# Router logits made token-major tile by tile, and the first expert block's rows selected by a one-hot product

## Chip, cores and metric

The kernel runs on one core of a Trainium2 chip. The metric is the device time of one execution, in microseconds (us), the median of three runs. The engines have short names in the profile: PE is the matrix engine, PEld its weight loads (which run beside its products), DVE the vector engine, ACT the scalar engine, POOL the GpSimd engine, SP the engine that issues most of the loads.

## The reference

A network of four layers works on 512 tokens of 768 features in f32. Each layer adds the outputs of a graph part, a mixing part and a feed-forward part to `x`. The change touches the feed-forward parts of layer 0 and layer 2, two mixtures of eight experts in which every token goes to the one expert with the largest logit. The one of layer 2, cut:

```python
x = hidden_states.reshape(-1, d)                 # normalized tokens, 512 x 768
logits = x @ Wg                                  # 768 x 8
probs = jax.nn.softmax(logits, axis=-1)
gate = jnp.max(probs, axis=-1)
expert_idx = jnp.argmax(probs, axis=-1)
h = jax.nn.silu(jnp.einsum('td,edf->etf', x, W1) + b1[:, None, :])   # 8 experts, 768 -> 384
y = jnp.einsum('etf,efd->etd', h, W2) + b2[:, None, :]               # 384 -> 768
combine = jax.nn.one_hot(expert_idx, e, dtype=x.dtype) * gate[:, None]
out = jnp.einsum('te,etd->td', combine, y)
```

Layer 0 has the same with a bias on the logits (`Ws`, `bs`) and gelu.

## The kernel before

Tokens lie in four tiles of 128 (`NT = 4`, `P = 128`). "Token-major" means tokens on the partitions (`xn`, 128 x 4 x 768); "feature-major" means features on the partitions in six chunks (`xnT`, 128 x 6 x 512, `KC = 6`). The routine `moe` (from line 1246) does both mixtures. Its first call, `"f0"` for layer 0, has a bias on the logits and a list of `fill` pieces: products for folding a graph part's weights (line 1787), placed between the routing's steps so that PE has work while DVE routes. Its second call, `"f2"` for layer 2, has no fills; its tokens' mean and spread are known already (`known=True`). The order on each engine is fixed when the program is built; `issue_after(last)` ties some PE pieces into a written order.

A call goes through these steps:

1. The tokens are normalized into `xn`, tile by tile (line 517 in call 1, lines 538 and 540 in call 2). `xn` is also written to memory as `there`, from which rows are gathered later, and in part as `back` (lines 1262 and 1264, from ACT's queue).
2. `to_fm` transposes all 24 128x128 blocks into six PSUM tiles of 512 columns, one per feature chunk, and then copies each out (`copy` alternates between DVE, line 290, and ACT, line 292).
3. `narrow` multiplies the gate's weights, padded to 32 columns, with `xnT` (line 437): the gate is the operand that is loaded, the tokens move, 512 at a time; the six chunks go to four column groups. DVE copies the result to `loT`, in call 1 with the bias. `narrow_tm` then turns it token-major with one product per tile against stacked identities (`fours`), and the logits are copied to `lo` (line 1275).
4. DVE finds each token's expert (maximum, first index), two bf16 products count the tokens per expert (`lower`, `onesb`; they wait for `gb`), and DVE works out `place`, the slot of each token in up to 11 blocks of 128 rows (`NB`), each block belonging to one expert, and `rows`, the row numbers of the blocks' weights. The fills 0 and 1 stand between these products on PE.
5. `spot` (line 1344) is a one-hot matrix in bf16, tokens against all 1408 slots, made tile by tile. 44 small products with token numbers (line 1349) turn it into `who`, the token of each slot. Fill 2 follows on PE.
6. POOL issues the loads with computed addresses, one after another in a written order (`send`): W1 of block 0, the rows of blocks 0 and 1 (`gather`, line 1411, from `there` by `who`), W1 of block 1, W2 of block 0, and so on (`pick`, line 1405).
7. For each block the gathered rows are transposed (`turned`), multiplied by W1 (`first`), transposed and put through the activation (`middle`), and multiplied by W2 (`second`). The block after is prepared meanwhile. Nine blocks always run (`NA`).
8. The results come back to token order and are added to `x`.

`acc` (line 429) is the product helper, `tr` (line 450) the transpose helper; most products in the profile stand under these two lines and are told apart by their tiles. `self.ones` is a 128x128 matrix of ones, `self.fours` four stacked 32x32 identities, `self.col(bs)` the bias with one expert on each partition.

Of the kernel before, what the change touches and what calls it, by code (L numbers as in the profile page):

```python
# [10 lines left out]
F32 = mybir.dt.float32  # L11
# [6 lines left out]
OP = mybir.AluOpType  # L18
# [4 lines left out]
P = 128  # L23
N = 512
NT = N // P
D = 768
KC = D // P
HW = 384
# [177 lines left out]
class Net:  # L206
# [250 lines left out]
    def to_fm(self, x, out):  # L457

        ps = [self.ps() for _ in range(KC)]
        for t in range(NT):  # L460
            for f in range(KC):
                self.tr(ps[f][:, t * P : (t + 1) * P], x[:, t, f * P : (f + 1) * P])
        for f in range(KC):
            self.copy(out[:, f, :], ps[f])

    def to_fm_last(self, x, out):

        nc, cut = self.nc, (NT - 1) * P
        ps = [self.ps() for _ in range(KC)]
        for t in range(NT - 1):  # L470
            for f in range(KC):
                self.tr(ps[f][:, t * P : (t + 1) * P], x[:, t, f * P : (f + 1) * P])
        for f in (0, 1, 3, 4):
            i = nc.scalar.copy(out[:, f, :cut], ps[f][:, :cut])
        with self.tc.issue_after(self.scaled):
            for f in (2, 5):
                nc.vector.tensor_copy(out[:, f, :cut], ps[f][:, :cut])
        for f in range(0, KC, 3):
            p = self.ps()
            for k in range(3):  # L480
                self.tr(p[:, k * P : (k + 1) * P], x[:, NT - 1, (f + k) * P : (f + k + 1) * P])
            at = out[:, f : f + 3, cut:], p[:, :HW].rearrange("p (k n) -> p k n", k=3)
            if f:
                nc.vector.tensor_copy(*at)
            else:
                with self.tc.issue_after(i.ins):
                    i = nc.scalar.copy(*at)
        return i.ins
# [757 lines left out]
    def moe(self, f, act, xn, xnT, wg, bs=None, fill=None, later=None, known=False):  # L1246
# [4 lines left out]
        nc, tc, d = self.nc, self.tc, self.d  # L1251
        E, NA, NB = 8, 9, NT + 7
        with ExitStack() as c:
            one = c.enter_context(tc.tile_pool(name=f + "_one", bufs=1))
            two = c.enter_context(tc.tile_pool(name=f + "_two", bufs=2))
# [6 lines left out]
            nc.scalar.dma_start(there.rearrange("(t p) d -> p t d", p=P), xn)  # L1262

            nc.scalar.dma_start(back[(NA - 1) * P :].rearrange("(t p) d -> p t d", p=P), xn[:, : NB - NA, :])
            self.to_fm(xn, xnT)
            xs = self.chunks(xnT)
            p = self.narrow(wg, xs)
            loT = one.tile([P, N], F32, name="loT")
            if bs is None:
                nc.vector.tensor_copy(loT, p)  # L1270
            else:
                nc.vector.tensor_scalar(loT, p, self.col(bs), None, OP.add)
            lo = one.tile([P, NT, E], F32, name="lo")
            logits = self.narrow_tm(loT, E)
            nc.vector.tensor_copy(lo, logits)
            last = self.told
            if fill:
                with tc.issue_after(last):
                    last = fill(0)
# [12 lines left out]
            p = self.ps()  # L1292
            gf = gb.rearrange("p t e -> p (t e)")
            with tc.issue_after(last):
                self.acc(p[:, :32], [(self.lower, gf)])
                last = self.acc(p[:, 32:64], [(self.onesb, gf)]).ins
            if fill:
                with tc.issue_after(last):
                    last = fill(1)
# [4 lines left out]
            n = cum[:, NT, :]  # L1304
# [16 lines left out]
            at = one.tile([P, NT, E], F32, name="at")  # L1321
# [3 lines left out]
            place = one.tile([P, NT, 1], F32, name="place")  # L1325
# [14 lines left out]
            spot = one.tile([P, NT, NB * P], BF16, name="spot")  # L1340
            io = one.tile([P, NB * P], I16, name="io")
            nc.gpsimd.iota(io, pattern=[[1, NB * P]], base=0, channel_multiplier=0)
            for t in range(NT):
                nc.vector.tensor_scalar(spot[:, t, :], io, place[:, t, :], None, OP.is_equal)
            p = self.ps()
            with tc.issue_after(last):
                for t in range(NT):
                    for i in range(NB):
                        last = nc.tensor.matmul(p[:, 2 * i : 2 * i + 2], spot[:, t, i * P : (i + 1) * P],
                                                self.number[:, t, :], start=t + i == 0,  # L1350
                                                stop=t == NT - 1 and i == NB - 1).ins
            if fill:
                with tc.issue_after(last):
                    last = fill(2)
            sums = one.tile([P, NB], F32, name="sums")
            nc.vector.tensor_reduce(sums, p[:, : 2 * NB].rearrange("p (i a) -> p i a", a=2), AX.X, OP.add)
            who = one.tile([P, NB], I32, name="who")
# [21 lines left out]
            p = self.ps()  # L1379
# [5 lines left out]
            p = self.ps()  # L1385
# [17 lines left out]
            def pick(table, i):  # L1403
                t = self.wp.tile([P, WB], F32, tag="w", name="w") if i < NA else two.tile([P, WB], F32, name="wm")
                return t, nc.gpsimd.indirect_dma_start(
                    out=t, out_offset=None, in_=table.rearrange("e p n -> (e p) n"),
                    in_offset=bass.IndirectOffsetOnAxis(ap=rows[:, i : i + 1], axis=0))

            def gather(i):
                xb = two.tile([P, D], F32, name="xb", bufs=3)  # L1410
                return xb, nc.gpsimd.indirect_dma_start(
                    out=xb, out_offset=None, in_=there, in_offset=bass.IndirectOffsetOnAxis(ap=who[:, i : i + 1], axis=0))
# [4 lines left out]
            def send(fn, *args):  # L1417

                nonlocal sent
                with tc.issue_after(sent) if sent else nullcontext():  # L1420
                    t, i = fn(*args)
                sent = i.ins
                return t

            def turned(xb):
                xbT = two.tile([P, KC, P], F32, name="xbT")
                for k in range(0, KC, 3):
                    p = self.ps()
                    for j in range(3):
                        self.tr(p[:, j * P : (j + 1) * P], xb[:, (k + j) * P : (k + j + 1) * P])  # L1430
                    self.copy(xbT[:, k : k + 3, :], p[:, :HW].rearrange("p (k n) -> p k n", k=3))
                return xbT

            def first(i, xbT, w1):
                p = self.ps()
                w1 = w1.rearrange("p (k n) -> p k n", k=KC)
                self.acc(p[:, :HW], [(xbT[:, k, :], w1[:, k, :]) for k in range(KC)])
                h = two.tile([P, HW], F32, name="h" if i < NA else "hm")
                self.copy(h, p[:, :HW])
                return h  # L1440
# [23 lines left out]
            count = nc.values_load(more[:1], min_val=4, max_val=NB)  # L1464

            w1 = send(pick, W1, 0)
            xb = send(gather, 0)
            ahead = send(gather, 1)
            h = first(0, turned(xb), w1)
            w1 = send(pick, W1, 1)  # L1470
            w2 = send(pick, W2, 0)
            xbT = turned(ahead)
            for i in range(NA - 1):
                hT = middle(i, h)
                h = first(i + 1, xbT, w1)
                if i + 2 < NA:
                    xb = send(gather, i + 2)
                    w1 = send(pick, W1, i + 2)
                after = send(pick, W2, i + 1)
                if i + 2 < NA:  # L1480
                    xbT = turned(xb)
# [7 lines left out]
            with tc.If(count > NA):  # L1489
                for i in range(NA, NB):  # L1490
                    xb, wa, wb = gather(i)[0], pick(W1, i)[0], pick(W2, i)[0]
                    second(i, middle(i, first(i, turned(xb), wa)), wb)
            ys = []
            for t in range(NT):
                ys.append(two.tile([P, D], F32, name="yb", bufs=NT))
                i = nc.gpsimd.indirect_dma_start(out=ys[t], out_offset=None, in_=back,
                                                 in_offset=bass.IndirectOffsetOnAxis(ap=slot[:, t : t + 1], axis=0))
# [11 lines left out]
            last = None  # L1509
# [18 lines left out]
            for t in range(NT):  # L1528
                x = self.x[:, t, :]
                for nb in range(2):  # L1530
                    at = slice(nb * HW, (nb + 1) * HW)
# [1370 lines left out]
```

## Time and profile before

| what | us |
|---|---|
| median of three runs | 3619.51 (3616.93 to 3624.39) |
| the profiled execution's own time | 3622.55 |
| its span | 3620.3 |
| mean granted PE clock | 0.992 |

A page of the profile gives busy times and shares by engine, then groups of instructions. A timeline gives, for each merged group, its start from the start of the span, how long it lasts, engine, line, operation, the tile written and those read, partitions and elements, the number of records (`x12`) and in brackets how long the engine had been idle and what released it. A stretch of time gives the busy time of PE, PEld, DVE, ACT and POOL with the number of instructions, then the granted PE clock (1.00 is full), the share of DMA time and GB/s. The first call's head lies at about 811 to 842 us, the second's at about 2171 to 2205.

### The profile page before, as it was taken

The numbers are of one execution on the slowest core, as the hardware profiler recorded it, in microseconds if no ns is written. First come the engines' busy times: TensorE is split into PE (matmuls) and PEld (weight loads), VectorE is DVE, ScalarE is ACT, GpSimd is POOL, SyncE is SP. The second block draws the span as 40 slices with busy tenths as digits, with TensorE's granted clock in tenths as the row PEclk, the third lists the DMA queues.
The fourth block names the chain that finished last, engine by engine and source line by source line (L and its number), as shares of the span: only waits on it lengthen the run. The fifth ranks groups of instructions, "written<-read, shape, count | busy, mean of one in ns | idle before, by whom it ended". The sixth has DMA issues, their size and how long they took to land. (4 is left out here: it accounts for less than half of the span.)

```text
span 3620.3 us, 40628 instructions
## 1 busy us (share of the span) xinstructions
PE 3526.4 (97%) x15976; PEld 2206.5 (61%) x15981; DVE 1699.7 (47%) x3407; ACT 985.6 (27%) x1753; POOL 475.2 (13%) x522
## 2 busy tenths in 40 slices
PE   8999999999999999999999998999999999999998
PEld 6767666655686675587888885555444444444444
DVE  8647664652523662366777763575222221221211
ACT  3533332432341443142343422363000000000000
POOL 8211110012003010001221213111000000000000
PEclk9999999999999999999999998999999999999999
DMA  4213112228322221032121118415999999999998
GB/s 179 90 50 130 48 71 93 80 95 332 105 79 82 72 114 35 0 110 100 54 90 66 66 40 316 144 53 211 393 424 424 424 424 424 424 424 424 424 425 359
DMA packets 100220, 714.56 MB, mean 197 GB/s; under 512 B 11904, under 2 KB 16256, under 8 KB 31024
## 3 DMA queue, kind: packets, MB, share of 16 engines
q1 hardware_dynamic: 79264, 604.81, 41.5%
q0 software_dynamic: 16848, 95.99, 7.0%
q10 hardware_dynamic: 3904, 11.01, 0.8%
q8 instruction: 132, 2.16, 0.2%
q14 instruction: 72, 0.59, 0.0%
HBM read 689.22 MB, written 22.54 MB: 197 GB/s over the span
## 5 line engine op out<-in xcount | busy, mean ns | idle before, releaser
L2703 PE MATMUL ps<-w,xg 128*64 128x384 f32 x3072 | 565.3, 489 | 6.4 <-DMA w<-in_f_Wg_dram 3.1
L2703 PEld LDWEIGHTS ps<-w,xg 128*64 128x64 f32 x3072 | 236.8, 137 | 294.1 <-issue 261.8
L429 PE MATMUL ps<-ops,w 128*128 128x512 f32 x1584 | 383.7, 392 | 0.7 <-POOL ops L2034 0.7
L429 PEld LDWEIGHTS ps<-ops,w 128*128 128x128 f32 x1584 | 296.0, 188 | 64.9 <-issue 1.9
L2719 PE MATMUL ps<-w,hT 128*64 128x384 f32 x1536 | 319.9, 490 | 3.0 <-DMA w<-in_f_Wd_dram 1.6
L2207 PE MATMUL ps<-ops,w 128*128 128x512 f32 x1080 | 258.9, 390 | 1.4 <-ACT ops L2103 0.9
L2706 ACT ACTIVATE h<-ps 128x384 f32<-128x384 f32 x64 | 31.5, 492 | 794.2 <-PE ps L2703 794.2
L2084 ACT ACTIVATE w<-w 128x768 fp32r<-128x768 f32 (+1 forms) x192 | 156.3, 823 | 316.7 <-PE ps L429 235.1
L2719 PEld LDWEIGHTS ps<-w,hT 128*64 128x64 f32 x1536 | 133.0, 137 | 162.4 <-issue 137.9
L2207 PEld LDWEIGHTS ps<-ops,w 128*128 128x128 f32 x1080 | 202.1, 188 | 45.5 <-ACT ops L2103 2.5
L522 DVE TENSOR_TENSOR x<-x,ps 128x384 f32<-128x384 f32 x224 | 122.9, 553 | 188.9 <-PE ps L429 180.5
L2128 DVE TENSOR_TENSOR w<-w,w 128x768 fp32r<-128x768 f32 x174 | 166.1, 958 | 82.0 <-ACT w L2084 78.7
L2707 DVE TENSOR_TENSOR h<-h,ps 128x384 f32<-128x384 f32 x64 | 35.4, 554 | 355.0 <-PE ps L2703 328.7
L429 PE MATMUL ps<-w,hT 128*128 128x384 f32 x552 | 184.6, 490 | 4.0 <-ACTq L1489 3.6
L429 PE MATMUL ps<-w,xnT 128*128 128x384 f32 x564 | 188.5, 488 | 0.0
L2098 POOL TENSOR_TENSOR low<-low,ops 128x512 f32<-128x512 f32 x90 | 118.6, 1317 | 422.0 <-ACT ops L2084 422.0
L2129 DVE SCALAR_TENSOR_TENSOR w<-w 128x768 fp32r<-128x768 f32 x174 | 170.8, 984 | 3.3
L429 PEld LDWEIGHTS ps<-w,hT 128*128 128x128 f32 x552 | 103.1, 190 | 81.5 <-ACT xbT L292 7.1
L429 PEld LDWEIGHTS ps<-w,xnT 128*128 128x128 f32 x564 | 106.6, 191 | 73.1 <-issue 5.1
L2660 PE MATMUL ps<-xnT,sw 128*128 128x512 f32 x288 | 135.4, 603 | 0.0
L429 PE MATMUL ps<-C,parts 128*128 128x512 f32 x576 | 132.5, 389 | 0.0
L2105 DVE TENSOR_TENSOR ops<-ops 128x512 fp32r<-128x512 f32 x138 | 123.9, 908 | 16.4 <-ACT ops L2103 16.0
(587 smaller groups left out, 5188.3 us busy)
## 6 DMA issues: line engine op xcount, KB each, us to landing
w<-in_f_Wg_dram SPq DMA_DIRECT2D x128, 1152.0 KB, 22.4
w<-in_f_Wu_dram SPq DMA_DIRECT2D x128, 1152.0 KB, 22.3
w<-in_f_Wd_dram SPq DMA_DIRECT2D x124, 1152.0 KB, 22.4
w<-in_g_w_dram SPq DMA_DIRECT2D x54, 1152.0 KB, 5.1
w<-in_m_wqkv_dram SPq DMA_DIRECT2D x16, 1152.0 KB, 6.3
w<-in_g_t_dram SPq DMA_DIRECT2D x12, 1152.0 KB, 5.1
w<-in_m_wp_dram SPq DMA_DIRECT2D x11, 1152.0 KB, 5.1
ea<-in_attr_dram SPq DMA_DIRECT2D x17, 512.0 KB, 4.8
```

The costliest lines, as they stand in the source:

```text
L429: i = self.nc.tensor.matmul(out, a, b, start=n == 0, stop=n == len(pairs) - 1)
L522: self.nc.vector.tensor_add(xs, xs, p)
L2084: return self.nc.scalar.activation(top, x, AF.Copy, scale=CUT).ins
L2098: (engine or nc.gpsimd).tensor_sub(low, v, ops[:, 0, k, :].bitcast(F32))
L2105: nc.vector.tensor_sub(dif, top.bitcast(F32), x.bitcast(F32))
L2128: nc.vector.tensor_sub(low, w, top.bitcast(F32))
L2129: self.sliced_last = nc.vector.scalar_tensor_tensor(dif, low.bitcast(F32), -TIMES, top.bitcast(F32), OP.mult, OP.add).ins
L2207: nc.tensor.matmul(outs[o], w[:, i, k], ops[:, i, k, :], start=n == 0 and i + k == 0, stop=n == 4 and i + k == KC)
L2660: i = nc.tensor.matmul(p, w[:, k, :], xnT[:, k, :], start=k == 0, stop=k == KC - 1)
L2703: nc.tensor.matmul(p[a * 64 : a * 64 + 64, :HW], xg[:, k, a * CAP : (a + 1) * CAP], ws[b][a][:, k, :], start=k == 0, stop=k == KC - 1)
L2707: nc.vector.tensor_mul(h, h, pu[:, :HW])
L2719: nc.tensor.matmul(po[nb][a * 64 : a * 64 + 64, :HW], hT[:, f * P + a * 64 : f * P + a * 64 + 64], wd[a][:, f, nb * HW : (nb + 1) * HW], s ...
```

## The change

It has two parts, both in `moe`, so that both calls have them.

*Logits.* `to_fm_tiles` takes the place of `to_fm`: a tile of tokens is transposed into two PSUM tiles of three blocks each, these are copied out at once (384 columns a copy, eight copies in all), and when the next tile's copies have been issued, `logit` makes the eight logits of the tile before. In that product the tokens of `xnT` (128 x 128) are the operand that is loaded and the gate's eight columns move. In call 1 the bias comes in as a seventh product, of the matrix of ones with `bsd`, the bias on a diagonal, made on POOL. `narrow`, `loT` and `narrow_tm` go.

*Rows of block 0.* `spot0` is the one-hot matrix of the first 128 slots in f32, made ahead of `spot`. `selected` multiplies `xn` by it, four tiles accumulated for each of six feature chunks, which gives block 0's rows feature-major in `xb0` at once. Chunks 0 to 2 come before the 44 small products on PE, chunks 3 to 5 after fill 2. The gather of block 0 and its six transposes go; block 1's gather follows W1 of block 0 on POOL.

```diff
+    def to_fm_tiles(self, x, out, done=None):
+        for t in range(NT):
+            for f in (0, 3):
+                p = self.ps()
+                for k in range(3):
+                    self.tr(p[:, k * P : (k + 1) * P], x[:, t, (f + k) * P : (f + k + 1) * P])
+                self.copy(out[:, f : f + 3, t * P : (t + 1) * P], p[:, :HW].rearrange("p (k n) -> p k n", k=3))
+            if done and t:
+                done(t - 1)
+        if done:
+            done(NT - 1)
...
-            self.to_fm(xn, xnT)
-            xs = self.chunks(xnT)
-            p = self.narrow(wg, xs)
-            loT = one.tile([P, N], F32, name="loT")
-            if bs is None:
-                nc.vector.tensor_copy(loT, p)
-            else:
-                nc.vector.tensor_scalar(loT, p, self.col(bs), None, OP.add)
+            if bs is not None:
+                bsd = one.tile([P, E], F32, name="bsd")
+                nc.gpsimd.tensor_scalar(bsd, self.fours[:, :E], self.col(bs), None, OP.mult)
+            logits = self.ps()
+            def logit(t):
+                pairs = [(xnT[:, k, t * P : (t + 1) * P], wg[:, k, :E]) for k in range(KC)]
+                if bs is not None:
+                    pairs.insert(0, (self.ones, bsd))
+                self.told = self.acc(logits[:, t * E : (t + 1) * E], pairs).ins
+            self.to_fm_tiles(xn, xnT, logit)
             lo = one.tile([P, NT, E], F32, name="lo")
-            logits = self.narrow_tm(loT, E)
-            nc.vector.tensor_copy(lo, logits)
+            nc.vector.tensor_copy(lo, logits[:, : NT * E].rearrange("p (t e) -> p t e", t=NT))
...
+            spot0 = one.tile([P, NT, P], F32, name="spot0")
+            nc.vector.tensor_tensor(spot0, io[:, None, :P].to_broadcast([P, NT, P]),
+                                    place.to_broadcast([P, NT, P]), OP.is_equal)
             for t in range(NT):
                 nc.vector.tensor_scalar(spot[:, t, :], io, place[:, t, :], None, OP.is_equal)
+            xb0 = two.tile([P, KC, P], F32, name="xbT")
+            def selected(k):
+                p = self.ps()
+                for j in range(3):
+                    at = slice((k + j) * P, (k + j + 1) * P)
+                    i = self.acc(p[:, j * P : (j + 1) * P], [(xn[:, t, at], spot0[:, t, :]) for t in range(NT)])
+                self.copy(xb0[:, k : k + 3, :], p[:, :HW].rearrange("p (k n) -> p k n", k=3))
+                return i.ins
+            with tc.issue_after(last):
+                last = selected(0)
             p = self.ps()
...
             if fill:
                 with tc.issue_after(last):
                     last = fill(2)
+            with tc.issue_after(last):
+                selected(3)
...
             w1 = send(pick, W1, 0)
-            xb = send(gather, 0)
             ahead = send(gather, 1)
-            h = first(0, turned(xb), w1)
+            h = first(0, xb0, w1)
```

## The prediction

> **What bounds the kernel now.** I read the page's busy shares first.
>
> ```profile
> span 3620.3 us, 40628 instructions
> PE 3526.4 (97%) x15976; PEld 2206.5 (61%) x15981; DVE 1699.7 (47%) x3407; ACT 985.6 (27%) x1753; POOL 475.2 (13%) x522
> ```
>
> PE works 97% of the span, so the change can only matter in the heads of the two mixture calls, and there by what PE and the chain behind it do. Next comes the timeline of the head of the first call (start, duration, engine, line, operation, in brackets the idle time before and its releaser):
>
> ```profile
> 811.02 0.56 POOL L454 DMA_DIRECT2D f_wg_gate<-in_f_wg_dram  x1 [31.26 <-issue]
> 812.25 1.53 PE L450 MATMUL ps<-ident,xn 128*128 128x128 f32 x12 [0.18 <-DVE xn L517]
> 814.79 0.88 PE L450 MATMUL ps<-ident,xn 128*128 128x128 f32 x6 [1.01 <-DVE xn L517]
> 817.38 1.91 PE L437 MATMUL ps<-xnT,f_wg_gate 128*32 128x512 f32 x12 [1.71 <-DMA f_wg_gate<-in_f_wg_dram]
> 820.14 1.06 PE L429 MATMUL ps<-fours,loT 128*128 128x8 f32 x8 [0.85 <-DVE loT L1272]
> 821.24 0.19 DVE L1275 COPY lo<-ps 128x32 f32<-128x32 f32 x1 [1.15 <-PE ps L429]
> ...
> 826.15 0.58 DVE L1344 TENSOR_SCALAR spot<-io,place 128x1408 bf16<-128x1408 int16 x1
> ...
> 828.97 5.76 PE L1787 MATMUL ps<-w,wq 128*32 128x384 f32 x36
> ...
> 836.42 4.14 PE L429 MATMUL ps<-w,xbT 128*128 128x384 f32 x12 [0.20 <-issue]
> ```
>
> Three things: the gate's weights land only about 817.3, when the old narrow product starts; each f32 product is two passes (12 records for six products, 8 for four); and the gathered rows cost call 1 nothing, since the fold products of L1787 fill that time. Call 2 has no fold products:
>
> ```profile
> 2174.71 4.53 PE L450 MATMUL ps<-ident,xn 128*128 128x128 f32 x24 [3.53 <-ACT xn L540]
> 2179.36 2.46 PE L437 MATMUL ps<-xnT,f_wg_gate 128*32 128x512 f32 x12
> 2183.70 0.19 DVE L1275 COPY lo<-ps 128x32 f32<-128x32 f32 x1 [1.15 <-PE ps L429]
> ...
> 2197.09 1.54 PE L450 MATMUL ps<-ident,xb 128*128 128x128 f32 x6 [2.71 <-DMA xb<-f_there,who]
> 2198.56 5.83 PE L429 MATMUL ps<-w,xbT 128*128 128x384 f32 x12
> ```
>
> Here the gather is on the path, by 2.71 us. The same 12 passes take 5.83 us instead of 4.14, so I asked for stretches of 3.41 us, the length of the half-clock stretch in call 1 (PE, PEld, DVE, ACT, POOL busy, then the granted clock):
>
> ```profile
> 826.43:829.84 3.41, 2.79 (x57) 2.04 (x60) 3.41 (x13) 0.00 (x0) 1.09 (x1) 1.00 0.43 110
> 829.84:833.25 3.41, 3.41 (x18) 1.02 (x15) 1.50 (x6) 0.00 (x0) 2.74 (x3) 0.50 0.91 327
> 2171.28:2174.69 3.41, 0.00 (x0) 0.00 (x0) 3.27 (x19) 2.00 (x6) 2.83 (x6) 1.00 0.15 40
> 2174.69:2178.11 3.42, 3.40 (x16) 3.16 (x17) 1.93 (x2) 0.89 (x1) 1.45 (x2) 0.50 0.47 164
> 939.10:942.50 3.40, 2.59 (x15) 2.29 (x13) 2.05 (x8) 1.92 (x5) 0.00 (x0) 0.50 0.00 0
> 842.20:924.70 82.50, 80.23 (x283) 47.02 (x284) 17.50 (x30) 20.15 (x49) 15.79 (x17) 1.00 0.87 329
> ```
>
> The clock halves for whole stretches after PE did little. In 826.43 to 829.84 PE shows 2.79 us busy, much of it products two columns wide, and still the clock fell: busy time alone doesn't hold it, width does. The last line is the expert loop: PE has 80.23 of 82.50 us, so a later first expert product moves the end one for one.
>
> **Prices.** A pass whose 128x128 f32 weights are loaded for 8 columns: eight loads took 0.97 us (timeline, L429 loT), 0.19 the last, so (0.97 - 0.19)/7 = 0.11 us. A transpose: (1.53 - 0.87)/6 = 0.11 us. At half clock transposes take 0.22 (six 1.54 against 0.82 us). A narrow pass at half clock isn't in the trace: from 0.11 (the load keeps its pace) to 0.22 (it halves). Large f32 loads lasted 0.34 us at half clock and 0.19 at full, so I take 0.22. A selection pass, 128 columns, is bounded by an f32 transpose (0.11) and a third of a 384-column pass (0.32/3): 0.11.
>
> **Logits, call 1.** Removed: the L437 product, loT (0.75 us) and the L429 product, 5.0 us from gate to lo less gaps. Added: 24 products and 4 bias products, 56 passes. The program order of the changed kernel puts the transposes of the last token tile behind the logits of tiles 0 to 2 and all bias products: 36 + 6 = 42 passes, which can't start before the gate's landing (the bias pass of tile 0 goes earlier). So 817.4 + 42 x 0.11 = 822.0; six transposes 0.65; a copy of 384 columns 0.56 with some 0.5 us of latencies, half under the transposes; 12 passes 1.3 and 0.26 to come out: lo at about 824.7, **+3.5**. That is with the clock at full. But between 813.7 and the fold products PE does only transposes of 0.65 us and 8-column passes. By this profile's grid the clock would fall at 819.6: 20 passes done, 22 x 0.22 = 4.8 to 824.4, transposes 1.3, copies 0.5, 12 x 0.22 = 2.6, 0.3: lo at 829.1, **+7.9**. Fallen from the start: 831.2, +10. I take +7.9. The first fold products (1.49 us at full clock) then hold up the count product that waits behind them, +0.7 at half clock.
>
> The bias operand on POOL and the 8 smaller copies in place of 6 lie in front of the gate's landing; without that cover, two 0.56 us copies ahead of tile 3's scaling. The write of the rows to memory comes some 1.4 us later; its first reader is 10 us away.
>
> **Logits, call 2.** The gate is there early. PE starts at 2174.71 with 24 transposes and 48 passes. With the clock as it was (half to 2178.11) lo comes at 2184.7, **+1.0**; at half throughout 24 x 0.21 + 48 x 0.22 = 15.6 us and 0.3, lo at 2190.6, **+7**. A half-clock stretch with 3.40 us of PE busy reopened the clock, one with 2.59 didn't; tiles 0 and 1 give 2.6 us of transposes, then narrow passes. Undecided: midpoint, **+4**.
>
> [...]
>
> **Selection.** Added per call: spot0 (0.71 us, the 128x512 tensor-tensor of L1612), 24 products of two passes (2 x 2.7 us), two copies. Removed: gather 0, its issue (1.4 us on POOL), six transposes. Call 1, from the start of spot (826.15) to the first expert product (836.42): 10.3 us before. After: 0.7 + 2.7 + counts 44 x 0.025 = 1.1 + fold 3.9 (full clock, the selection being wide; 5.8 if not) + 2.7 + 0.7 of small transposes + 0.3 = 12.1, **+1.8** (to +3.7). Gather 0 was under the fold, so nothing comes back.
> Call 2: before, lo to the end of the first product is 2204.4 - 2183.7 = 20.7. After: 5.6 to spot0, some 5.1 of selection mostly at half clock, 1.2 counts, 2.7, 0.7, 4.4: 19.7, **-1**. But the count product stands behind the first selection, so gather 1, and behind it on POOL the second block's weights, are issued some 2.7 us later against lo (who 4 later, one issue of 1.4 less); in the old run they came 10 us before use, landing after about 8: some 1 us of wait, **+1**. Net 0.
>
> **Sum.** Call 1: 7.9 + 0.7 + 1.8 = 10.4; call 2: 4 + 0; together **+14.4 us** (from 6.3 at full clock to 14.4 + 7 = 21). Nothing behind absorbs it: the last stage is loads as buffers come free. On the profiled execution's own 3622.55 us, 3637; it lies 3.0 over the median of the runs, so on the median **3634**.
>
> **Rivals.** *The clock stays open*: 8-column passes with their loads count as work. For: load records nearly fill PE. Against: the stretch 826.43. 5.3 + 1.0 = +6.3: 3626. *Weights late in call 2*: the second block's waits in full, for it speaks DMA at 0.9 and more of its time there; another +3 to +4: 3638. *Not slower*: the gate lands 2.3 us after issue as the other small loads do when queues are empty, so the logits vanish under the normalization (lo -0.2), the selection opens the clock for call 2 (-3.3 against +1.0), and the 3.2 us between first and second expert product of call 1 shrink to call 2's 1.1: -0.2 + 1.8 - 2.3 - 2.1 = -2.8, 3617. It decides if the gate lands before 814. Against: DMA busy share 0.97 in 812.8 to 816.2. *The gather is not gone*: excluded, POOL's program order has one gather less in each call.
>
> **Numbers.** Forecast 0.55, clock open 0.25, weights late 0.10, not slower 0.10. Two tenths of a per cent, 7.2 us, is about what a measurement of this kernel can tell from none. Slower by more: 0.55 + 0.10 + 0.02 of the open clock; within: 0.23 + 0.03; faster by more: 0.07. Range 3620 to 3643: from the open clock less 2 of that pause and some scatter (the runs span 7.5 us) to both calls at half clock.
>
> **What would show it.** Lo at 824 to 831 in call 1 with half clock in the logits; 42 narrow passes behind the gate's landing; first expert product of call 1 starting 8 to 14 us later; in call 2 no wait for gather 0. Wrong if lo of call 1 comes before 823, or if the narrow passes run at 0.05 us.

## The result and the profile after

| | before | after |
|---|---|---|
| median of nine runs each, us | 3620.1 (3615.84 to 3628.86) | 3639.53 (3630.33 to 3646.72) |
| ratio, 95% interval | | 1.005 (1.0041 to 1.0059) |
| span of the profiled execution, us | 3620.3 | 3635.8 |

The changed kernel is slower by 0.5%, 18 us by the ratio (15 to 21). First the page, engines with busy time, share and instructions:

```profile
span 3635.8 us, 40923 instructions
PE 3547.6 (98%) x16124; PEld 2232.5 (61%) x16129; DVE 1699.2 (47%) x3409; ACT 985.6 (27%) x1755; POOL 473.5 (13%) x521
```

PE is busy for 21.2 us more and the span is 15.5 longer; VectorE, ScalarE and GpSimd do no more than before. So I looked on PE itself first, for more work or a slower pace. The timeline of call 1's head (start, duration, engine, line, operation, idle time before and its releaser):

```profile
814.80 2.70 PE L429 MATMUL ps<-f_wg_gate,xnT 128*128 128x8 f32 x12 [3.17 <-DMA f_wg_gate<-in_f_wg_dram]
...
817.77 2.71 PE L429 MATMUL ps<-f_wg_gate,xnT 128*128 128x8 f32 x12
...
820.76 2.71 PE L429 MATMUL ps<-f_wg_gate,xnT 128*128 128x8 f32 x12
...
823.75 1.52 PE L450 MATMUL ps<-ident,xn 128*128 128x128 f32 x6
...
825.28 2.73 PE L429 MATMUL ps<-f_wg_gate,xnT 128*128 128x8 f32 x12
828.05 0.19 DVE L1291 COPY lo<-ps 128x32 f32<-128x32 f32 x1 [2.82 <-PE ps L429]
...
834.76 2.94 PE L429 MATMUL ps<-spot,xn 128*128 128x128 f32 x24 [0.77 <-DVE spot L1360]
...
846.15 1.46 PE L429 MATMUL ps<-w,xbT 128*128 128x384 f32 x4
```

These lines show that the logits of three tiles stand one behind another after the gate's landing, that tile 3's transposes come only then, and that twelve narrow passes last 2.71 us: starts lie 0.213 apart, twice the 0.11 of the full clock. The stretches say so too (PE, PEld, DVE, ACT, POOL busy, granted clock, share of DMA time, GB/s):

```profile
811.17:814.58 3.41, 0.46 (x5) 0.22 (x3) 1.96 (x6) 1.04 (x3) 0.00 (x0) 1.00 0.99 331
814.58:817.99 3.41, 3.19 (x16) 3.22 (x16) 0.00 (x0) 0.00 (x0) 0.00 (x0) 0.50 1.03 417
817.99:821.41 3.42, 3.42 (x18) 3.42 (x18) 0.00 (x0) 0.00 (x0) 0.00 (x0) 0.50 0.33 135
...
828.23:831.65 3.42, 3.42 (x20) 0.90 (x17) 2.05 (x15) 0.23 (x1) 0.00 (x0) 0.50 0.03 7
831.65:835.06 3.41, 2.64 (x26) 0.89 (x19) 3.20 (x21) 0.00 (x0) 0.64 (x1) 1.00 0.00 0
```

The clock had halved before the first narrow pass, after a stretch spent mostly waiting for the gate. In the kernel before, the stretch ahead of the gate's landing held the transposes of tile 3 too, and the clock stayed:

```profile
812.77:816.19 3.42, 1.89 (x16) 1.41 (x14) 2.56 (x7) 1.22 (x3) 0.00 (x0) 1.00 0.97 308
```

Full stretches of narrow passes (3.42 of 3.42 us) didn't open it; the first stretch of wide fold products, 828.23, did. Call 2:

```profile
2182.10 2.93 PE L450 MATMUL ps<-ident,xn 128*128 128x128 f32 x12 [3.52 <-ACT xn L553]
2185.03 2.73 PE L429 MATMUL ps<-f_wg_gate,xnT 128*128 128x8 f32 x12
...
2192.66 5.13 PE L429 MATMUL ps<-f_wg_gate,xnT 128*128 128x8 f32 x24
2197.82 0.19 DVE L1291 COPY lo<-ps 128x32 f32<-128x32 f32 x1 [4.36 <-PE ps L429]
...
2203.51 4.69 PE L429 MATMUL ps<-spot,xn 128*128 128x128 f32 x24 [3.86 <-DVE spot L1360]
...
2209.15 2.92 PE L429 MATMUL ps<-spot,xn 128*128 128x128 f32 x24
...
2219.39 4.11 PE L429 MATMUL ps<-w,xbT 128*128 128x384 f32 x12 [1.46 <-DMA w<-in_f_w_dram,rows]
```

Everything up to 2207.22 runs at half clock (the first selection takes 4.69 us, the second 2.92 for the same 24 passes). The wait of 2.71 us for gathered rows is gone, and a new one of 1.46 us stands ahead of the second expert product: W1 of block 1.

For all kernels below, three marks of each call, in us from the call's own first transpose of `xn`: the copy to `lo`, the first expert product, and the first product with `wayT`, which closes the expert loop.

| kernel | call 1: lo | first | wayT | call 2: lo | first | wayT | ratio to before, 95% |
|---|---|---|---|---|---|---|---|
| before | 10.0 | 25.2 | 115.5 | 9.0 | 23.9 | 114.8 | |
| after | 19.2 | 37.3 | 125.0 | 15.7 | 30.5 | 121.3 | 1.005 (1.0041 to 1.0059) |
| e1_rows_only | 9.7 | 26.8 | 120.0 | 9.5 | 24.6 | 115.5 | 1.0008 (0.9999 to 1.0017) |
| e2_logits_only | 18.7 | 34.4 | 121.8 | 15.7 | 30.5 | 121.3 | 1.0036 (1.0023 to 1.0049) |
| e3_wide_between | 19.8 | 38.4 | 128.2 | 15.7 | 30.2 | 122.4 | 1.006 (1.0043 to 1.0077) |
| e4_gate_early | 13.4 | 31.6 | 123.3 | 15.7 | 30.4 | 123.3 | 1.004 (1.0026 to 1.0055) |
| e5_token_major | 15.0 | 33.2 | 123.2 | 13.7 | 29.2 | 120.2 | 1.0046 (1.0031 to 1.0062) |
| e6_hold_second | 19.6 | 37.7 | 127.7 | 27.9 | 42.4 | 133.5 | 1.0116 (1.01 to 1.0133) |
| e7_rows_second | 11.0 | 26.2 | 116.4 | 9.2 | 24.9 | 113.6 | 1.0004 (0.9995 to 1.0013) |
| e8_warm_before | 9.6 | 24.2 | 118.8 | 13.8 | 33.3 | 124.1 | 1.004 (1.0026 to 1.0054) |
| e9_warm_sized | 10.0 | 24.7 | 112.9 | 8.0 | 22.9 | 113.9 | 1.0 (0.9991 to 1.0009) |
| e10_second_warm_gate | 8.9 | 23.5 | 112.6 | 8.0 | 21.0 | 110.4 | 0.998 (0.9971 to 0.9989) |
| e11_second_warm | 9.6 | 24.6 | 112.8 | 8.0 | 21.0 | 110.4 | 0.9984 (0.9975 to 0.9993) |
| e12_changed_warm | 19.1 | 37.2 | 124.7 | 12.8 | 26.6 | 117.3 | 1.0051 (1.0037 to 1.0064) |

After less before: call 1 +9.5 at wayT, call 2 +6.5, sum 16.0 of the 15.5 us by which the spans differ. Marks come from one execution each, and wayT scatters. Five kernels have the call 1 of before (before, e7, e8, e9, e11): 112.8 to 118.8 at wayT, 115.3 in the mean. Three have the changed one (after, e6, e12): 124.7 to 127.7, mean 125.8. Three have the changed call 2 (after, e3, e4): 121.3 to 123.3, mean 122.4. So two or three us at wayT are not the edit's unless the trace shows where they went. The means give +10.5 for call 1 and, against the one profile of the old call 2, +7.5: together the 18 us of the ratio. Up to the first expert product a call repeats better, within 0.6 us in the changed call 1, 0.3 in the changed call 2 and 2 in the old call 1.

### The profile page after: what moved, and what is told of

Its sections match the earlier page's. It is cut to its first block, busy times and chain, and to the rows that moved or that the text cites. A ratio compares the mean times of both kernels' runs of the same rounds, so it can differ in the third digit from the quotient of the medians.

```text
span 3635.8 us, 40923 instructions
## 1 busy us (share of the span) xinstructions
PE 3547.6 (98%) x16124; PEld 2232.5 (61%) x16129; DVE 1699.2 (47%) x3409; ACT 985.6 (27%) x1755; POOL 473.5 (13%) x521
## 4 chain that ended last, share of the span: by engine, by line
PE 82%; DMA 7%; DVE 6%; issue 2%; ACT 1%; POOL 1%; DVEq 0%; POOLq 0%; ACTq 0%; SPq 0%
PE ps L429 45%; PE ps L2735 11%; PE ps L2239 6%; PE ps L2751 6%; PE ps L450 3%; PE ps L2692 3%; DMA w<-in_f_Wu_dram 2%; PE ps L1063 2%; DMA w<-in_f_Wd_dram 2%; DMA w<-in_f_Wg_dram 2%; PE ps L1935 2%; PE ps L400 1%; PE ps L1916 1%; PE ps L668 1%; DVE pt L1645 1%
## 5 line engine op out<-in xcount | busy, mean ns | idle before, releaser
L2137 DVE TENSOR_TENSOR ops<-ops 128x512 fp32r<-128x512 f32 x138 | 123.8, 907 | 16.4 <-ACT ops L2135 15.7
```

The costliest lines, as they stand in the source:

```text
L2137: nc.vector.tensor_sub(dif, top.bitcast(F32), x.bitcast(F32))
```

## The experiments

**The two parts apart.** e1 keeps the selection and has the old logits, e2 the reverse.

```diff
 # e1_rows_only, from the changed kernel
-            self.to_fm_tiles(xn, xnT, logit)
+            self.to_fm(xn, xnT)
+            p = self.narrow(wg, self.chunks(xnT))
...
 # e2_logits_only, from the changed kernel
+            xb = send(gather, 0)
-            h = first(0, xb0, w1)
+            h = first(0, turned(xb), w1)
```

> The selection alone, with the old logits. Theory (the loss is the narrow passes at half clock): lo stays where it was before, 10.2 us behind the issue of the gate's load in call 1 and 10.0 in call 2; the first expert product of call 1 starts about 2 us later than before, the second one within 1 us; time within 5 us of before, ratio 0.998 to 1.002. Rival (the selection's 24 f32 products on PE are the loss): 8 us or more slower, ratio over 1.002.

> The token-major logits alone, with the old gather of block 0. Theory: lo 19 us behind the issue of the gate's load in call 1 (10.2 before) and 13 to 17 in call 2 (10.0), nearly all of it kept to the end: 13 to 19 us slower, ratio 1.0035 to 1.0055. Rival (selection is the loss): under 6 us slower.

Measured: 3626.93 against 3621.54 us for the selection alone, 1.0008; 3636.44 us and 1.0036 for the logits alone. The logits carry the loss: lo late by 8.7 and 6.7 us, as in the changed kernel. The selection isn't a gain (1.0008 is 2.9 us, interval 0 to 6). In call 1 of e1 lo to the first product takes 17.05 us against 15.19, the +1.8 of the prediction, and behind that stands a wait that wasn't in it:

```profile
837.44 0.60 PE L450 MATMUL ps<-ident,g 128*8 128x128 f32 x4
...
838.09 1.46 PE L429 MATMUL ps<-w,xbT 128*128 128x384 f32 x4
...
840.12 0.68 DVE L1412 COPY gT<-ps 8x512 f32<-8x512 f32 x1 [7.78 <-PE ps L429]
...
841.05 0.33 PE L450 MATMUL ps<-ident,way 128*128 128x128 f32 x1 [1.50 <-DVE way L1418]
841.86 0.33 PE L450 MATMUL ps<-ident,way 128*128 128x128 f32 x1 [0.48 <-issue]
```

DVE makes the third `way` tile behind its copy of `gT`, and that copy starts at 840.12, 2.1 us after PE has made the transposes that it reads (838.04); PE waits for the tile inside its first expert product. Call 1's code alone doesn't make the pause: call 1 of e3, e4, e5 and e6 has it (1.5 to 1.6 us at the third tile), but the changed kernel and e12, whose call 1 is the same code as e6's, don't; in the changed kernel the copy starts with the end of the transposes (846.13). No run shows what decides it.

**The clock in call 1.** e3 puts wide bf16 products, whose result nobody reads, among the logits of call 1; e4 loads call 1's gate ahead of the attention before it.

```diff
 # e3_wide_between, in logit(t), behind every second of the seven products
+                            self.told = nc.tensor.matmul(spare, self.onesb,
+                                self.onesb[:, None, :].to_broadcast([P, NT, P]), start=True, stop=True).ins
...
 # e4_gate_early
+        gate0 = net.gate_of(gl.enter_context(tc.tile_pool(name="L1g", bufs=1)), "f0_wg")
         net.attention0(nodesT, bv0)
```

> The changed kernel with 16 added bf16 products, 512 columns wide and of no use, one after every second narrow product of call 1's logits. Theory (the clock falls because the products are narrow): the clock stays at 1.00 there, a narrow pass takes 0.11 us instead of 0.22, and in spite of 16 more products of about 0.24 us lo of call 1 comes 16.5 to 18.5 us behind the issue of the gate's load instead of 19.4. Rival (the passes are slow for another reason, the load of f32 weights or transfers beside them): passes stay at 0.22 us and lo comes at 23 us or later.

> The changed kernel with call 1's gate loaded ahead of the attention before it, into a place of its own. Theory (the logits of call 1 start at the gate's landing): PE doesn't wait 3.2 us for the gate, some 20 passes run before the clock falls, and lo comes 4 to 6 us earlier against the first transpose than in the changed kernel; time 3 to 7 us under it. Rival (the last tile's normalization or the copies set lo): lo within 1.5 us of the changed kernel's.

e3 missed: the clock fell all the same, 8.2 us after the first transpose, and lo came at 19.8. Before the fall its narrow passes started 0.112 us apart, after it 0.214, so the pace is the clock's. The stretch at whose end it fell (816.55 to 819.96) held 0.9 us of the wait for the gate and only four of the sixteen wide products, and in the stretches behind it the rest didn't open it again. e4 did what was expected of lo, 5.8 us earlier, and shows the cause of the fall by itself, since there PE waited for nothing (stretches as above):

```profile
813.70:817.12 3.42, 3.42 (x34) 3.37 (x32) 2.38 (x7) 1.04 (x3) 0.00 (x0) 1.00 0.99 363
817.12:820.53 3.41, 3.41 (x18) 3.41 (x18) 0.00 (x0) 0.00 (x0) 0.00 (x0) 0.50 1.03 417
```

A stretch at the full clock, busy to the last hundredth with narrow passes and a few transposes, is followed by half clock. Only 1.7 of e4's 5.7 us at the first product are left at wayT: the pause at `way` stands in this profile (1.61 and 0.40 us) and not in the changed kernel's, and a half-clock stretch of 3.4 us fell at 847.81, onto the expert products. The total, 3637.38 against 3639.53 us, is 2 us less, where 3 to 7 were expected; the runs can't tell that from nothing.

**Interleaving or narrowness.** e5 undoes "tile by tile" and keeps "token-major".

```diff
-            self.to_fm_tiles(xn, xnT, logit)
+            self.to_fm(xn, xnT)
+            for t in range(NT):
+                logit(t)
```

> The changed kernel, but with all 24 transposes of xn made first, as before the change, and the 48 token-major passes of the logits behind them: tile by tile is undone, token-major is kept. Theory (the narrow passes and their half clock are the loss, not the interleaving): in call 1 the transposes fit into the wait for the gate, the 56 passes then run at 0.214 us each, 12.0 us from +5.9, so lo at +18.0 after the first transpose (19.2 in the changed kernel, 10.0 before); in call 2 24 transposes at 0.11 to 0.21 us and 48 passes at 0.214 give +14 to +16 (15.7 changed, 9.0 before); ratio to before 1.0035 to 1.006. Rival (the interleaving of two kinds of work, and the half-size copies, cost the time): lo back at +10 to +13 in both calls, ratio under 1.002.

Measured 3637.23 us, 1.0046. Lo came at 15.0 and 13.7, earlier than I had expected (18.0, and 14 to 16), as part of the passes ran at the full clock (in call 1 half only from +8.4 to +18.7). That is between the theory's price and the rival's in call 1, but the total is the theory's: the narrow passes are most of the loss. Interleaving them adds 4.2 and 2.0 us to lo in these profiles; the 1.8 and 1.1 left at wayT are within its scatter, and the totals can't tell them from nothing (1.005 against 1.0046).

**Holding the clock in call 2.** e6 and e8 fill call 2's waits (and, in e6, its logits) with f32 products of 512 columns that nobody reads, e6 in the changed kernel, e8 in the one before.

```diff
 # both, at the end of the graph part ahead of call 2, 8 times
                     leave(5, 6)
+                            self.last_tr = nc.tensor.matmul(spare, self.ident, xnT[:, KC - 1, :], start=True, stop=True).ins
...
 # e6, in logit(t) of call 2, behind every third pass; e8 has 3, 8 and 6 behind the logits, the count and the table
+                            self.told = nc.tensor.matmul(spare, self.ident, xn[:, t, :512], start=True, stop=True).ins
```

> The changed kernel with wide f32 products of 512 columns whose result nobody reads, on TensorE in call 2 alone: 8 of them in the 3.5 us wait ahead of the first transpose, and one behind every third narrow pass that follows its fellows (8 more). Theory (the clock falls because narrow passes and the wait ahead of them put little width through TensorE; wide work holds it): no half clock until lo of call 2, the passes at 0.112 us in place of 0.214, lo at 24 x 0.11 + 48 x 0.112 + 8 x 0.43 = 11.5 us, plus 0.5 of waits, +12 after the first transpose against +15.7, and the call 3 to 4 us shorter at its first expert product. Rival (the passes are paced by loading 128 x 128 weights, whatever the clock, or the clock falls all the same): passes stay at 0.214 and lo moves to +15.7 + 3.4 to 6 = +19 to +22, time 3 to 6 us above the changed kernel.

> The kernel before with wide f32 products of 512 columns that nobody reads in the waits of call 2 alone: 8 ahead of the first transpose, 3 behind the logits, 8 behind the running count, 6 behind the block table. Nothing of the change is in it; it prices the half clock by itself. Theory (idle waits drop the clock, and the half clock is what the stage then pays): no half clock in call 2 from the first transpose on; transposes 2.65 us in place of 4.53, first expert product 4.1 in place of 5.8, its rows' transposes 0.8 in place of 1.5; call 2 shorter by 3 to 5 us up to its products with wayT, ratio 0.9985 to 0.9993. Rival (the stage is set by VectorE, GpSimd and the gather's landing, and TensorE's clock is paid only in its own cover): transposes shorter but the products with wayT less than 1 us earlier, ratio 0.9995 to 1.0008.

Both are misses of mine: an f32 product is two passes of 0.44 us, which the prediction had read off the profile for other products, so eight took 7 us in a wait of 3.5; and the gate's load was issued 7.1 us later, counted from the graph part's last transposes, probably because it goes into memory that the reading of `xnT` held. Ratios of 1.0116 and 1.004 say nothing of the clock. One thing is left: in e8 the 24 transposes took 2.84 us instead of 4.53. e9 repeats e8 with bf16 products of ones, cut to the waits (14, 6 and 15), and e12 puts the same ones into the changed kernel.

```diff
 # e9_warm_sized and e12_changed_warm
+    def wide(self, last, n):
+        p = self.ps()
+        b = self.onesb[:, None, :].to_broadcast([P, NT, P])
+        for _ in range(n):
+            with self.tc.issue_after(last):
+                last = self.nc.tensor.matmul(p, self.onesb, b, start=True, stop=True).ins
+        return last
...
                     leave(5, 6)
+                    self.wide(self.last_tr, 14)
...
                     last = fill(0)
+            else:
+                last = self.wide(last, 6)
...
                     last = fill(1)
+            else:
+                last = self.wide(last, 15)
```

> The kernel before with bf16 products of 512 columns (0.215 us each at the full clock) that nobody reads, in call 2 alone and cut to the waits: 14 ahead of the first transpose (3.0 us in a wait of 3.5), 6 behind the logits (1.3 in 1.6), 15 behind the running count (3.2 in 3.75). The f32 products tried for this took 0.44 us for each of two passes and overran the waits; these don't. Theory (the half clock is what call 2's stage pays): no half clock from the first transpose to the first expert product, transposes 2.7 us in place of 4.5, gate product and way transposes shorter, call 2 shorter by 2.5 to 4.5 us at its products with wayT (112.3 or less to 110.3 after the first transpose, 114.8 before); ratio 0.9985 to 0.9995. Rival (VectorE, GpSimd and the gather set the stage behind lo, so only the transposes count): first expert product 1.5 to 2.2 us earlier and no more, ratio 0.9993 to 1.0002.

> The changed kernel whole, with the same wide bf16 products in call 2's waits (14 ahead of the first transpose, 6 behind the logits, 15 behind the running count). Theory (half of call 2's loss is the clock, half the number of passes): the clock is open at the first transpose; the narrow passes put so little width through TensorE that it falls after one or two of its windows of 3.41 us, so that the first 20 to 40 passes run at 0.112 and the rest at 0.214: lo at +11 to +14 (15.7 changed, 9.0 before), the call 3 to 6 us shorter at its products with wayT (121.3 changed), ratio to before 1.002 to 1.0045. Were the clock open throughout, lo would be at 24 x 0.11 + 48 x 0.112 and 1.2 of waits = +9.2: then the passes themselves cost nothing against before. Rival (the clock falls at once all the same): lo at +15 to +16, ratio 1.0045 to 1.006.

e12's logits in call 2, and two stretches of them:

```profile
2184.94 1.50 PE L429 MATMUL ps<-f_wg_gate,xnT 128*128 128x8 f32 x12 [0.67 <-ACT xnT L292]
...
2189.66 5.13 PE L429 MATMUL ps<-f_wg_gate,xnT 128*128 128x8 f32 x24
```

```profile
2181.30:2184.72 3.42, 1.94 (x13) 1.28 (x12) 3.39 (x7) 1.88 (x3) 2.14 (x3) 1.00 0.27 88
2184.72:2188.13 3.41, 3.19 (x29) 3.20 (x30) 0.70 (x2) 1.02 (x3) 0.00 (x0) 1.00 1.02 389
2188.13:2191.54 3.41, 3.41 (x19) 3.41 (x18) 0.56 (x1) 1.76 (x2) 0.00 (x0) 0.50 0.65 253
```

After 1.94 us, twelve transposes and the end of one wide product, the clock stays open; after 3.19 us, most of them narrow passes, it falls. Twelve passes take 1.50 us while the clock is open and half of 5.13 once it has fallen, 6.1 us after the first transpose. Lo came at 12.8, within the range expected, the first expert product 3.8 and wayT 4.0 us earlier than in the changed kernel. The total is 1.0051, where 1.002 to 1.0045 was expected; the interval of its five runs (1.0037 to 1.0064) reaches into that, and the medians (3638.21 against 3622.11 us) make 1.0044. The profile shows the gain in call 2; that the whole kernel is faster for it isn't shown, and isn't excluded.

e9 fell on the rival's side: lo and the first product 1 us earlier (the rival had 1.5 to 2.2) and the total 1.0. Its transposes run at 0.11, but the clock falls again at 2185.88, after a stretch of products two columns wide, a few small transposes and short waits. The wait for the gathered rows follows, and the first expert product pays:

```profile
2182.47:2185.88 3.41, 2.23 (x40) 1.53 (x37) 3.41 (x14) 0.00 (x0) 0.68 (x2) 1.00 0.68 211
```

```profile
2189.93 1.51 PE L450 MATMUL ps<-ident,xb 128*128 128x128 f32 x6 [2.72 <-DMA xb<-f_there,who]
2191.36 6.48 PE L429 MATMUL ps<-w,xbT 128*128 128x384 f32 x12
```

**The part that can win.** e7 has the selection in call 2 alone, old logits in both calls, and W1 of block 1 issued ahead of the rows of block 1. e11 adds e9's wide products, e10 also the early gate.

```diff
 # e7_rows_second, call 2
-            ahead = send(gather, 1)
-            h = first(0, xb0, w1)
-            w1 = send(pick, W1, 1)
+            after = send(pick, W1, 1)
+            ahead = send(gather, 1)
+            h = first(0, xb0, w1)
+            w1 = after
```

> The kernel before with the one-hot selection in call 2 alone (call 1 keeps its row gather, both calls keep the old logits), and with W1 of the second block picked ahead of the gather for that block on GpSimd's queue. Theory: with the selection in both calls, call 2 waited 1.24 us for W1 of block 1 and 0.73 us for its rows, and ended 0.7 us later than before from its first transpose; W1 issued first takes the 1.24 us away and the rows come up to 1 us later, so call 2 ends -0.5 to +0.5 us against before and the ratio is 0.9995 to 1.0005. Rival (the rows wait grows by what the weights wait loses, and more): rows wait over 1.7 us, ratio over 1.0005.

> Three things that single runs showed to shorten a call, put together: the one-hot selection in call 2 alone with W1 of the second block first (call 2 was 1.2 us shorter), the gate of call 1 loaded ahead of the attention before it (old logits; the wait of 1.7 us for it goes), and the wide bf16 products in call 2's waits (14, 6 and 15 as in the run beside it). Theory: call 2 at its products with wayT at 108 to 111 us after its first transpose (114.8 before, 113.6 with the selection alone), call 1 at 114 to 115.5 (115.5 before); together 4 to 8 us, ratio 0.9978 to 0.9990. Rival (each gain is taken back by the next wait: W2 of the first block, rows of the second, the way transposes on VectorE): call 2 no better than 112.5, call 1 at 115.5 or later, ratio 0.9992 to 1.0005.

> The kernel that ran at 0.998 of before, without its early gate: the one-hot selection in call 2 alone, W1 of the second block first, and the wide bf16 products in call 2's waits. Call 1 is the one of before. Theory (the selection is work that stands where the gather's wait was, and with wide products around it the clock stays open through the stage; each alone gave 1 us in call 2): call 2 at 110 to 111 us at its products with wayT, no half clock in it, and call 1 at 115.5 as before but for its own clock: ratio 0.9983 to 0.9992. Rival (the 0.998 came from call 1's gate): call 2 at 112.5 or later, ratio 0.9995 to 1.0005.

e7: 1.0004, no difference that can be measured; call 2's waits for W1 and rows are gone, but its first selection runs at half clock, and the 1.2 us less at wayT are within the scatter:

```profile
2191.33 5.46 PE L429 MATMUL ps<-spot,xn 128*128 128x128 f32 x24 [3.95 <-DVE left L1346]
```

For e10 and e11 the totals are clear of before's: 3615.47 against 3622.32 us, 0.998, and 3615.4 against 3622.11, 0.9984. Both are faster than both kernels by a little. Call 2 is 4.4 us shorter in both, which fits e11's ratio (5.8 us, interval 2.5 to 9), and the early gate adds nothing that can be seen (e11 without it is as fast). In e11:

```profile
2178.97 3.40 PE L464 MATMUL ps<-onesb 128*128 128x512 bf16 x15
2182.98 2.94 PE L429 MATMUL ps<-spot,xn 128*128 128x128 f32 x24 [0.61 <-DVE spot L1372]
...
2186.87 2.92 PE L429 MATMUL ps<-spot,xn 128*128 128x128 f32 x24
```

Selection stands where the gather's wait stood, at the full clock, and no half-clock stretch is left in the call up to wayT. At call 2's first expert product, the mark that repeats, the selection alone was 1.0 us later than before and the wide products alone 0.9 earlier; together they are 2.9 earlier. Each keeps open what the other needs: the wide products the clock for the selection (2.94 us in place of e7's 5.46), the selection the clock up to the expert product (its twelve passes take 4.2 us in place of e9's 6.48).

## Why the prediction was right, and where it was off

It named slower, for the right reason (narrow passes behind the gate's landing, at half clock), at 3634 us; 3639.5 was measured, inside the range. It was +14.4 against some 18: in both calls the clock was at half from the start of the logits, which by the prediction's own upper cases is 10 + 0.7 + 1.8 + 7 = 19.5. By its steps:

- *Prices.* Right. A narrow pass takes 0.112 us at full clock and 0.214 at half (0.11 and 0.22 taken), 24 selection passes 2.94 and a selection matrix 0.69. One reading was off, without use in the sum: from the gate to lo the rows of before give 3.9 us (817.38 to 821.24), not 5.0.
- *Logits, call 1, +7.9.* Measured +9.1. The order was right: 42 passes behind the landing and ahead of tile 3's transposes. The grid, the times at which the stretches end, was off: the clock was to fall at 819.6, with 20 passes done; it fell at 814.58, in the wait for the gate, which is the step's own upper case, "Fallen from the start", +10. The step took the wait's own stretch for harmless. In before it held tile 3's transposes (814.79; 1.89 us of PE in 812.77 to 816.19); the change moves them behind the logits, and 0.46 us were left (811.17 to 814.58). Of the 9.1, 54 passes x 0.102 us and six transposes x 0.105 are the clock, 6.1; the other 3.0 is the step's full-clock case, +3.5.
- *Logits, call 2, midpoint +4.* The mis-sized term: +6.7, near its upper end of +7. The clock was at half from 2.2 us before the first transpose until past lo; six transposes (2179.91 to 2183.32, 1.22 us of PE), then eight transposes and eight narrow passes (2183.32 to 2186.74, 3.41 us) didn't open it, where in before sixteen transposes did (2174.69 to 2178.11, 3.40 us). 48 passes x 0.102 = 4.9 of it is the clock, and e12, with the clock open at the start, takes 2.9 of the 6.7 away.
- *Transposes and the clock.* In e12 the stretch 2181.30 to 2184.72 holds twelve transposes and at most 0.2 us of wide products (those ahead of the first transpose ended by 2181.50), and the clock stays open. In the changed kernel a stretch of eighteen narrow passes, 817.99 to 821.41, busy throughout, left the clock at half.
- *Selection, call 1, +1.8.* +1.86 in e1. *First fold, +0.7:* 0.5 in e2 (lo to first product 15.7 us against 15.2), 1.05 by the changed kernel less e1.
- *Selection, call 2, net 0.* From lo to wayT 105.6 us against 105.8: net -0.2. The two halves were larger than taken: W1 of block 1 cost 1.46 and the rows 0.51, against +1, and the first expert product was back at the full clock (its twelve passes take 4.2 us, 5.83 before).
- *Sum.* Call 1: +12.1 at the first product against 10.4, but +9.5 at wayT (+10.5 in the means). The pauses of 1.01 and 0.81 us between the first and second expert product of the old call 1 are gone, so "Nothing behind absorbs it" was too strong; the prediction had that pause only in a rival and in the range's lower end. Call 2: +6.5 against 4. The upper end "14.4 + 7 = 21" counts call 2's 4 twice; with 7 in its place it is 17.4, and 19.5 with call 1's +10 as well.
- *Rivals.* *The clock stays open:* refuted (half from 814.58 to 831.65). *Weights late in full:* about half of its price came, 1.46 + 0.51 us. *Not slower:* its condition, the gate landing early, was made true in e4, and the kernel was still slower (1.004): with the gate there, the clock fell all the same, at 817.12, after a stretch of 34 passes, most of them narrow, that left PE no gap (3.42 of 3.42 us).

Open: what makes the parts behind the marks differ. From call 2's wayT to the end, which no edit touches, the fourteen profiles take 1330.7 to 1337.9 us; in e12's it is 2.8 us more than in the changed kernel's, so its span shows only 1.3 of the 4.0 us. Open too is what makes the pause at `way`.

## What to carry to other kernels

Count a product by its passes, not by its being short: here a narrow pass, eight columns moved, took 0.112 us at the full clock and 0.214 at half, as much as a transpose, which moves 128 (0.11 and 0.22), and after a stretch made mostly of them the clock fell for the passes that followed (e4, 817.12). Work that took the place of a wait gained here when the clock was open for it (the selection in call 2: 2.94 us in e11, 5.46 in e7) and when the chain around it was moved with it (the weights queued behind the rows cost 1.46 us in the changed kernel, no wait in e7). Price a moved product in passes before sizing anything by it: e6's eight f32 products of 512 columns were sixteen passes and took 7 us in a wait of 3.5.

## What the runs showed of the hardware that I had not expected

That PE, busy without a gap in the profile, lost its clock (e4, 3.42 of 3.42 us), or didn't get it back (the changed kernel, 817.99 to 828.23, 10.23 of 10.24 us), while, busy for 1.94 of 3.42 us, PE kept it (e12, 2181.30 to 2184.72). So busy time as the profile counts it doesn't sort these stretches. What passed through PE in these stretches, and the granted clock behind them:

| stretch | clock in it | PE busy, us | passes | clock behind it |
|---|---|---|---|---|
| e4, 813.70 to 817.12 | 1.00 | 3.42 | 34, six or seven transposes, the others narrow | 0.50 |
| e12, 2181.30 to 2184.72 | 1.00 | 1.94 | 12 transposes, the end of a wide product | 1.00 |
| before, 826.43 to 829.84 | 1.00 | 2.79 | 44 of two columns, 4 transposes of `g`, 9 fold passes of 384 | 0.50 |
| after, 817.99 to 821.41 | 0.50 | 3.42 | 18 narrow | 0.50 |
| after, 2183.32 to 2186.74 | 0.50 | 3.41 | 8 transposes, 8 narrow | 0.50 |
| before, 2174.69 to 2178.11 | 0.50 | 3.40 | 16 transposes | 1.00 |
| after, 828.23 to 831.65 | 0.50 | 3.42 | 18 fold passes of 384, 2 of 32 | 1.00 |

The prediction's "width does" was an estimate from the third row. Among the stretches of transposes and narrow passes the wider ones kept or opened the clock, but no run shows that width is the measure: the columns moved, counted plainly, don't order all rows, since the third moved more than the second or the sixth.
